# Attention with image prompts on one core: the inner products of the tokens of batches one to seven computed in four 32-column tiles of TensorE

## The chip, the cores and the metric

The kernel runs on one core of one Trainium2 chip. The metric is the device time of one execution in microseconds (us). The kernel before takes 440.3 us, the median of three executions (440.11, 440.3 and 442.06).

## The reference

Eight batches. Each has 112 query tokens of 320 channels (`hidden_states`) and 375 context tokens of 512 channels; the last 4 context tokens are image prompts, the 371 others are text. There are 20 heads of 16 channels. All is in fp32.

```python
q = heads(hidden_states @ W_q); k_t = heads(text_ehs @ W_k); v_t = heads(text_ehs @ W_v)
probs_t = softmax(q k_t^T * attn_scale)
text_out = probs_t @ v_t
attn_scores = q @ heads(ip_ehs @ W_k_ip)^T * attn_scale
qsem = l2norm(einsum('bhst,bte->bhse', probs_t, text_ehs))
sem  = einsum('bhse,bne->bhsn', qsem, l2norm(ip_ehs))
probs_ip = softmax(attn_scores + 0.5 * sem) * spatial_mask
out = (text_out + probs_ip @ heads(ip_ehs @ W_v_ip)) @ W_out + b_out + hidden_states
```

`qsem` is a vector of 512 channels for each head and query. The kernel never forms it. Its length is a quadratic form in the probabilities, with the matrix of the inner products of all text tokens with each other (the Gram matrix, 371 x 371), and its products with the prompts are the probabilities times the inner products of text and prompts. So a batch needs one matrix G of 375 columns: inner products of its tokens with its tokens, the last four columns being the normalised prompts.

## The kernel before, in words

G is symmetric, so only its upper triangle is used, with the elements off the diagonal doubled and those on it halved against that. The 375 tokens, padded to 384, are 12 blocks of 32. Block j is needed from its own first column to column 375: 375 - 32 j columns.

**The products (`gram`, L450 to L467).** `ctxT` holds the context turned round: channels on the 128 partitions, in four pieces e of 128 channels, tokens along the free dimension. For each chunk c of 128 tokens (4 blocks) four matmuls, one for each e, add up a tile of 128 tokens x (375 - 128 c) columns in a PSUM bank of its own: 375, 247 and 119 columns. The stationary operand is the chunk (128 columns), so the whole 128x128 array is used, and for three blocks in four also columns are computed that lie below the triangle. Banks come from a pool of two (`ps_mm`). `doubled` (L442) follows each chunk: ScalarE writes twice the bank into `ug` in SBUF, GpSimd multiplies the square at the diagonal by a mask `half` that holds 0.5 in the 32x32 blocks at the diagonal and 1.0 elsewhere. An fp32 matmul appears in the profile as two instructions, with a weight load each, and is called two passes here: `gram` has 24 passes for a batch.

**What it feeds.** `gram_to_groups` (L469) copies each 32 rows of `ug` by DMA to the four groups of 32 partitions of the tile `u`; `placed` (L600, GpSimd) puts the values of a group of heads behind them. `multiplied` (L679 to L699) is the largest stage: for 5 groups of 4 heads in each batch and 12 blocks of tokens, matmuls on four tiles of 32 rows at once (L692), block j with 392 - 32 j columns. Then VectorE multiplies each result with the probabilities and adds up (`reduced`, L740), ScalarE copies the sums out (`value_sums`, L705).

**What sets the order.** PE, SP and VectorE run in the order in which the program text issues instructions, ScalarE too after the prologue (`manual_schedule`); GpSimd's order is chosen by the framework's scheduler until the last batch. One step (b, g) of the main loop (L1125) issues: the 48 matmuls of `multiplied`, with the scores of the group two steps on (L637) after blocks 0 and 6, their maxima (L650, VectorE), exponentials (L654, ScalarE) and DMAs of the probabilities (L663, SP), the transpose for the next step after block 2 (L673, VectorE), `value_sums`, `reduced`, `placed`, and then `between(b, g)` (L1025), which puts other work between two steps: after g = 0 the `gram` of the next batch, after g = 1 and 2 its `values` (L531) and `keys` (L497), after g = 3 and 4 keys, queries and the output of earlier batches. Batch 0 has its own `first_gram` in the prologue (L420, on `ps_qd` banks), and after its first step `prompt_projections` (L264) runs among the chunks of batch 1's `gram`: eight matmuls that write 32 partitions each, two side by side at different partitions (L273), and then three small transposes (L289).

Of the kernel before, what the change touches and what calls it, by code (L numbers as in the profile page):

```python
# [20 lines left out]
def kernel(  # L21
# [14 lines left out]
    nc = tc.nc  # L36
# [28 lines left out]
    GCOL = [sum(WC[:c]) for c in range(NT + 1)]  # L65
    GW = GCOL[NT]
    UCOL = QN * GW
    assert (H, D, NC, NT, P) == (20, 16, 3, 3, 128) and RG == 2 * D


# [12 lines left out]
    def bank(name, spare=False):  # L83

        if spare:
            return ps_sc.tile([P, 512], F32, tag="sc", name=name)
        return ps_mm.tile([P, 512], F32, tag="mm", name=name)
# [80 lines left out]
    make_identity(nc, ident)  # L168
    nc.gpsimd.memset(wq_sb[REST:, FULL, :], 0.0)

    half = const.tile([P, P], F32, tag="half", name="half")
    nc.gpsimd.memset(half, 1.0)
    for q in range(QN):
        nc.gpsimd.memset(half[q * RG : (q + 1) * RG, q * RG : (q + 1) * RG], 0.5)

    hmask = const.tile([P, HC], F32, tag="hmask", name="hmask")
    nc.vector.tensor_reduce(
# [179 lines left out]
    def begin(b):  # L357
# [12 lines left out]
        s["pvs"] = work.tile([S, H, VW], F32, tag="pvs", name=f"pvs_{b}")  # L370
        s["vip"] = work.tile([S, NIP, H, D], F32, tag="vipb", name=f"vip_{b}")

    def region(b, c):

        u = st[b]["u"].rearrange("p (q w) -> p q w", w=GW)
        return u[:, :, GCOL[c] : GCOL[c + 1]]
# [38 lines left out]
    def warm(ps, n):  # L415

        for _ in range(n):
            nc.tensor.matmul(ps[:, NC * P :], ident, ident, start=True, stop=True)

    def first_gram():  # L420

        ctxT = st[0]["ctxT"]
        banks = []
        for c in range(NT):
            banks.append(ps_qd.tile([P, 512], F32, tag="qd", name=f"ps_g_0_{c}"))
            if c == NT - 1:
                nc.gpsimd.tensor_copy(ctxT[:, :, TT:T], ipnT[:, :, :NIP])
            c0, c1 = c * P, min(c * P + P, T)
            for r in range(c + 1):
                for e in range(NE):  # L430
                    nc.tensor.matmul(
                        banks[r][:, c0 - r * P : c1 - r * P],
                        ctxT[:, e, r * P : (r + 1) * P],
                        ctxT[:, e, c0:c1],
                        start=(e == 0),
                        stop=(e == NE - 1),
                    )
                if c == NT - 1:
                    doubled(banks[r], r)
                yield  # L440

    def doubled(ps, c):  # L442

        t0 = c * P
        k = min(P, TT - t0)
        g = ug[:, GCOL[c] : GCOL[c] + T - t0]
        nc.scalar.mul(g, ps[:, : T - t0], 2.0)
        nc.gpsimd.tensor_tensor(g[:, :k], g[:, :k], half[:, :k], ALU.mult)

    def gram(b):  # L450

        ctxT = st[b]["ctxT"]

        nc.gpsimd.tensor_copy(ctxT[:, :, TT:T], ipnT[:, :, b * NIP : (b + 1) * NIP])
        for c in range(NT):
            t0 = c * P
            ps = bank(f"ps_g_{b}_{c}")
            for e in range(NE):
                nc.tensor.matmul(  # L459
                    ps[:, : T - t0],  # L460
                    ctxT[:, e, t0 : t0 + P],
                    ctxT[:, e, t0:T],
                    start=(e == 0),
                    stop=(e == NE - 1),
                )
            doubled(ps, c)
            yield  # L467

    def gram_to_groups(b, blocks):  # L469
# [130 lines left out]
    def placed(b, g, chunks=range(NT)):  # L600

        s = st[b]
        for c in chunks:
            nc.gpsimd.tensor_copy(  # L604
                region(b, c)[:, :, UV - c * P :], s["vr"][:, c * QN : (c + 1) * QN, g, :]
            )

    def prompt_logits(b):

# [69 lines left out]
    def multiplied(b, g):  # L679
        s = st[b]  # L680
        xT = s.pop(("xT", g))
        banks = []
        for a in range(GROUP):

            if b == B - 1 and g % 2 and g < NG - 1:
                banks.append(bank(f"ps_qd_{b}_{g}_{a}", spare=a > 1))
            else:
                banks.append(ps_qd.tile([P, 512], F32, tag="qd", name=f"ps_qd_{b}_{g}_{a}"))
        for j in range(BLK):
            c, q = j // QN, j % QN  # L690
            for a in range(GROUP):
                nc.tensor.matmul(  # L692
                    banks[a][:S, j * RG : UW],
                    xT[a * RG : (a + 1) * RG, j, :S],
                    region(b, c)[a * RG : (a + 1) * RG, q, q * RG :],
                    start=(j == 0),
                    stop=(j == BLK - 1),
                )
            yield  # L699
        s["qd", g] = banks  # L700
# [317 lines left out]
    def run(key, make, pieces=1):  # L1018

        if key not in gens:  # L1020
            gens[key] = make()
        for _ in range(pieces):
            next(gens[key], None)

    def between(b, g):  # L1025

        nb = b + 1
        new = nb < B


        first = [bs for bs in pairs if bs[0] == (nb if b == 0 else nb + 1)]
        rest = [bs for bs in pairs if bs[0] == nb]
        if g == 0:
            if new:
                run(("g", nb), lambda: gram(nb), 2)
            if b == 0:
                run(("pp",), prompt_projections)
            if new:
                run(("g", nb), None)
            if b == 0:  # L1040
                run(("pp",), None)
            if b > 0 and new:
                run(("f", b - 1), lambda: finish(b - 1))
        if g == 1:
            if new:
                run(("v", nb), lambda: values(nb), 2)
            for bs in first if b == 0 else ():
                run(("q", bs[0]), lambda: project_queries(bs), 3)
        if g == 2 and new:
            run(("v", nb), None)  # L1050
            run(("k", nb), lambda: keys(nb))
            for bs in first if b == 0 else ():
                run(("q", bs[0]), None)
        if g == 2 and b > 0 and new:
            run(("f", b - 1), None, 2)
        if g == 3:
            if new:
                run(("k", nb), None, 1)
            if b > 0 and new:
                run(("f", b - 1), None)  # L1060
            for bs in first if b > 0 else ():
                run(("q", bs[0]), lambda: project_queries(bs), 3)
            if b == 0:
                run(("t", b), lambda: prompt_logits(b))
            for bs in rest:
                run(("q", bs[0]), None)
        if 0 <= g - (b == 0) < NT and nb + 1 < B:
            run(("c", nb + 1), lambda: transposed_context(nb + 1))
        if g == 4:
            if b > 0 and new:  # L1070
                run(("f", b - 1), None, 2)
            if nb < B - 1:
                run(("k", nb), None, 1)
            for bs in (first if b > 0 else []) + rest:
                run(("q", bs[0]), None)
# [49 lines left out]
    for n, (b, g) in enumerate(steps[:-NG]):  # L1125
        coming = steps[n + LEAD]
        for j, _ in enumerate(multiplied(b, g)):
            for a in {0: (2, 3), 6: (0, 1)}.get(j, ()):
                scores(*coming, a)
                if j == 0:  # L1130
                    probabilities(*coming, a)
            if j == 2:
                transposed(*steps[n + 1])
                if 1 <= g <= 3:
                    gram_to_groups(b + 1, {1: (0,), 2: (2,), 3: (3,)}[g])

                if g in (1, 2) and b > 0:
                    run(("f", b - 1), None)
        value_sums(b, g)
        if g == 2 and b > 0:  # L1140
            run(("f", b - 1), None)
        for a in (0, 1):
            probabilities(*coming, a)
        if n == len(steps) - NG - 1:
            sums = shared(b, g, GROUP // 2)
            next(sums)
            reduced(b, g, 2)
        else:
            reduced(b, g)
        placed(*steps[n + 1])  # L1150
        if g == 0 and b > 1:
            run(("f", b - 2), None)
        if n == 0:
            load_next(b + 2)
        if g == NG - 1:
            load_next(b + 3)
        if g == 1:
            gram_to_groups(b + 1, (1,))
        elif g == 3:
            values_to_groups(b + 1)  # L1160
        if g == 1 and b == 0:
            run(("pp",), None)
        if (b, g) == (B - 3, 1):
            prompt_values_by_head()
        if (b, g) == (B - 2, 1):
            bd = load_prompt_values_by_head()
        if g == NG - 1 and b < B - 2:
            prompt_values(b)
        between(b, g)
        if g == 1:  # L1170
            values_to_dram(b + 1, nc.sync, 0, 2)
        if g == 2:
            values_to_dram(b + 1, nc.sync, 2)
# [145 lines left out]
```

## Time and profile before

| | |
|---|---|
| median of three executions | 440.3 us |
| profiled execution, its own time | 440.06 us |
| its span, first to last instruction | 438.3 us |
| PE busy | 97% of the span |
| VectorE, ScalarE, GpSimd busy | 74%, 43%, 25% |
| granted TensorE clock | 1.000 |
| `gram` matmuls (L459) | 168 passes, 37.6 us busy |
| `multiplied` matmuls (L692) | 3840 passes, 219.6 us busy |

How to read it: the program is a long chain of steps on PE with the other engines beside it. Busy times of PE overlap, since matmuls are pipelined and tiles work side by side, so the length of a stage is read from the start of its first instruction to the start of the next stage's first one. "Idle before" in a group's line tells how long its engine stood idle just ahead of its instructions and what ended that.

### The profile page before, as it was taken

The page shows a single profiled execution, that of the slowest core. Times are in us where ns is not written, and L with a number is a line of the kernel's source. Part 1 is how long each engine was busy: PE and PEld are TensorE (multiplying, and loading weights), DVE is VectorE, ACT ScalarE, POOL GpSimd, SP SyncE. Part 2 cuts the span into 40 slices and gives each one's busy share as a digit, 9 for nine tenths or more (in the row PEclk, how much of TensorE's full clock was granted, in tenths as well). Part 3 has the DMA queues.
Part 4 walks back from the last instruction along what each step waited for, and adds up shares of the span by engine and source line. Part 5 has one row for each costly group of instructions (what it writes and reads, how often), then busy time and mean ns, then how long its engine had stood idle before and what let it go on. Part 6 is the DMA issues. An engine that isn't in the chain of part 4 may idle for free. (4 is left out here: it accounts for less than half of the span.)

```text
span 438.3 us, 12947 instructions
## 1 busy us (share of the span) xinstructions
PE 425.3 (97%) x5017; PEld 327.1 (75%) x5017; DVE 325.2 (74%) x669; ACT 189.2 (43%) x649; POOL 110.8 (25%) x268
## 2 busy tenths in 40 slices
PE   8998999989999999999999999999999999999976
PEld 8757767878777877788777877778777887776773
DVE  3047386887797878897797977887797877878774
ACT  2253333335344353334435353323534353336783
POOL 4301201012160211511152121511133121527340
PEclk9999999999999999999999999999999999999999
DMA  7669955674645946575646846467556527553300
GB/s 239 171 183 265 207 141 153 144 180 111 171 120 137 207 120 165 127 161 126 173 119 156 193 104 169 119 151 177 131 167 145 148 85 187 139 139 108 91 3 28
DMA packets 57611, 64.22 MB, mean 146 GB/s; under 512 B 18432, under 2 KB 51576, under 8 KB 57550
## 3 DMA queue, kind: packets, MB, share of 16 engines
q1 hardware_dynamic: 56984, 62.66, 57.0%
q8 instruction: 40, 0.66, 0.7%
q10 hardware_dynamic: 566, 0.72, 0.5%
q14 instruction: 21, 0.17, 0.1%
HBM read 18.67 MB, written 5.32 MB: 55 GB/s over the span
## 5 line engine op out<-in xcount | busy, mean ns | idle before, releaser
L692 PE MATMUL ps_qd<-u,xgT 32*112 32x328 f32 (+11 forms) x3840 | 219.6, 353 | 2.2 <-DVE xgT L673 1.2
L692 PEld LDWEIGHTS ps_qd<-u,xgT 32*112 32x112 f32 x3840 | 187.1, 172 | 35.2 <-issue 9.8
L673 DVE STREAM_TRANSPOSE xgT<-xg 128x1536 f32<-128x1536 f32 (+1 forms) x45 | 119.1, 2663 | 12.2 <-DMA xg<-p 8.1
L654 ACT ACTIVATE p<-ps_s,nmx 112x371 f32<-112x371 f32 x160 | 87.3, 584 | 86.9 <-DVE nmx L650 64.2
L650 DVE TENSOR_REDUCE nmx<-ps_s 112x1 f32<-112x371 f32 x160 | 77.8, 529 | 47.4 <-PE ps_s L637 46.2
L740 DVE CUSTOM_DVE_ANT_0 junk<-ps_qd,p 112x371 f32<-112x371 f32 x148 | 80.3, 543 | 15.7 <-ACT vext L538 0.5
L637 PE MATMUL ps_s<-kT,qm 32*112 32x375 f32 (+1 forms) x320 | 67.7, 484 | 1.0 <-ACT shared L723 0.7
L604 POOL COPY u<-vr 128x64 f32<-128x64 f32 x120 | 25.9, 237 | 151.9 <-PE ps_qd L692 102.6
L531 PE MATMUL ps_v<-wv_sb,ctxT 128*128 128x384 f32 (+1 forms) x192 | 63.5, 480 | 0.0
L531 PEld LDWEIGHTS ps_v<-wv_sb,ctxT 128*128 128x128 f32 x192 | 35.2, 190 | 19.7
L497 PE MATMUL ps_k<-ctxT,wk_sb 128*128 128x371 f32 x136 | 45.9, 482 | 0.0
L705 ACT COPY pvs<-ps_qd 112x21 f32<-112x21 f32 x150 | 16.0, 189 | 65.9 <-PE ps_qd L692 65.0
L459 PE MATMUL ps_g<-ctxT 128*128 128x375 f32 (+2 forms) x168 | 37.6, 380 | 0.0
L497 PEld LDWEIGHTS ps_k<-ctxT,wk_sb 128*128 128x128 f32 x136 | 25.1, 190 | 15.3 <-issue 0.5
L459 PEld LDWEIGHTS ps_g<-ctxT 128*128 128x128 f32 x168 | 28.0, 190 | 8.8 <-issue 0.5
L637 PEld LDWEIGHTS ps_s<-kT,qm 32*112 32x112 f32 x320 | 27.0, 170 | 6.9 <-ACT kT L504 2.1
L656 ACT COPY ipl<-ps_s 112x4 f32<-112x4 f32 x140 | 23.9, 170 | 0.0
L343 DVE TENSOR_SCALAR qm<-ps_q,emask 128x224 f32<-128x224 f32 (+1 forms) x25 | 9.1, 398 | 19.1 <-PE ps_q L334 19.0
L538 ACT COPY vext<-ps_v 128x384 f32<-128x384 f32 (+1 forms) x24 | 11.2, 468 | 22.8 <-PE ps_v L531 22.8
L386 DVE STREAM_TRANSPOSE ctxT<-ct 128x512 f32<-128x512 f32 x18 | 19.9, 1104 | 0.1
L504 ACT COPY kT<-ps_k 128x371 f32<-128x371 f32 x17 | 8.0, 469 | 25.2 <-PE ps_k L497 25.2
L883 POOL TENSOR_TENSOR wv<-vip,w 112x1280 f32<-112x1280 f32 x6 | 14.8, 2468 | 15.0 <-DVE w L823 15.0
(164 smaller groups left out, 313.8 us busy)
## 6 DMA issues: line engine op xcount, KB each, us to landing
xg<-p SPq DMA_DIRECT2D x159, 162.3 KB
u<-ug SPq DMA_DIRECT2D x128, 99.0 KB
ct<-in_ctx_dram SPq DMA_DIRECT2D x24, 176.0 KB
vr<-vd SPq DMA_DIRECT2D x32, 120.0 KB
vip<-vipd SPq DMA_DIRECT2D x6, 560.0 KB
vd<-vext SPq DMA_DIRECT2D x7, 320.0 KB
vd<-vext SPq DMA_DIRECT2D x7, 160.0 KB
out_dram<-ob SPq DMA_DIRECT2D x8, 140.0 KB
```

The lines of the kernel that those rows point to most:

```text
L386: nc.vector.transpose(ctxT[:, :, c * P : (c + 1) * P].rearrange("p e (j i) -> p j e i", i=RG), ct[:, some, :].rearrange("p j (k e) -> p j ...
L459: nc.tensor.matmul(ps[:, : T - t0], ctxT[:, e, t0 : t0 + P], ctxT[:, e, t0:T], start=(e == 0), stop=(e == NE - 1),)
L497: nc.tensor.matmul(ps[:, :TT], wk_sb[:, e, i * P : (i + 1) * P], s["ctxT"][:, e, :TT], start=(e == 0), stop=(e == NE - 1),)
L531: nc.tensor.matmul(ps[:, :w], ctxT[:, e, c * P : (c + 1) * P], wv_sb[:, e, :w], start=(e == 0), stop=(e == NE - 1),)
L604: nc.gpsimd.tensor_copy(region(b, c)[:, :, UV - c * P :], s["vr"][:, c * QN : (c + 1) * QN, g, :])
L637: nc.tensor.matmul(ps[:S, :w], qm[a * RG : (a + 1) * RG, i, r, j * S : (j + 1) * S], s["kT"][a * RG : (a + 1) * RG, i, :w], start=True, st ...
L650: nc.vector.tensor_reduce(nmx, ps[:S, :TT], AX.X, ALU.max, negate=True)
L654: nc.scalar.activation(p, ps[:S, :TT], AF.Exp, bias=nmx)
L656: nc.scalar.copy(s["ipl"][:, groups[g][a], :], ps[:S, TT:T])
L673: nc.vector.transpose(xT[:, j : j + n].rearrange("p j (k q) -> p q j k", q=QN), xg[:, :, j * RG : (j + n) * RG].rearrange("p q (j k) -> p ...
L692: nc.tensor.matmul(banks[a][:S, j * RG : UW], xT[a * RG : (a + 1) * RG, j, :S], region(b, c)[a * RG : (a + 1) * RG, q, q * RG :], start=(j ...
L740: nc.vector.tensor_tensor_reduce(out=junk, in0=ps[:S, :TT], in1=s["p", g][:, a, :], scale=1.0, scalar=0.0, op0=ALU.mult, op1=ALU.add, accu ...
```

## The change

`gram` is rewritten for batches 1 to 7. The stationary operand is one block of 32 tokens instead of a chunk of 128, and the result goes to the 32 partitions of column tile q (q = 0 to 3); the moving operand starts at the block's own first column. The 12 blocks are dealt to the four tiles by a table, and the matmuls of the tiles are issued in the order of the column count at which each tile would reach them. Chunks 1 and 2 share one bank. Parts of the banks that no matmul writes are set to zero by ScalarE (`cleared`) in block 2 of the step before. The masks, `placed` and `multiplied` follow the new order of blocks. In batch 0, the second and third piece of `prompt_projections` move by one place each: behind the steps (0, 1) and (0, 2).

```diff
+    BLOCKS = [[0, 1, 2, 3], [6, 7, 4, 5], [10, 8, 11, 9]]
+    PLACE = {j: (c, q) for c, js in enumerate(BLOCKS) for q, j in enumerate(js)}
...
-    half = const.tile([P, P], F32, tag="half", name="half")
+    half = const.tile([P, NT, P], F32, tag="half", name="half")
     nc.gpsimd.memset(half, 1.0)
-    for q in range(QN):
-        nc.gpsimd.memset(half[q * RG : (q + 1) * RG, q * RG : (q + 1) * RG], 0.5)
+    for c, js in enumerate(BLOCKS):
+        for q, j in enumerate(js):
+            nc.gpsimd.memset(
+                half[q * RG : (q + 1) * RG, c, (j - c * QN) * RG : (j - c * QN + 1) * RG], 0.5
+            )
...
+    def dealt(b, c, t):
+
+        if b == 0 or c == 0:
+            return t
+        v = t.rearrange("p (a b) w -> p a b w", a=2)
+        if c == 1:
+            return v[:, ::-1]
+        return v.rearrange("p a b w -> p b a w")[:, :, ::-1]
...
+    def cleared(ps, n=1):
+
+        w = P - RG
+        o = ps.rearrange("p (x w) -> p x w", w=2 * P)[:, :n, :w]
+        nc.scalar.mul(o, half[:, :n, :w], 0.0)
...
+    def gram_banks(b):
+
+        st["ps_g", b] = ps = [bank(f"ps_g_{b}_{c}") for c in range(2)]
+        for n, t in enumerate(ps):
+            cleared(t, n + 1)
...
-        for c in range(NT):
-            t0 = c * P
-            ps = bank(f"ps_g_{b}_{c}")
-            for e in range(NE):
-                nc.tensor.matmul(
-                    ps[:, : T - t0],
-                    ctxT[:, e, t0 : t0 + P],
-                    ctxT[:, e, t0:T],
-                    start=(e == 0),
-                    stop=(e == NE - 1),
-                )
-            doubled(ps, c)
+        ps = st.pop(("ps_g", b))
+        ps.append(ps[1][:, 2 * P :])
+
+        todo = []
+        for q in range(QN):
+            begun = 0
+            for c in range(NT):
+                for e in range(NE):
+                    todo.append((begun, c, q, e))
+                    begun += T - BLOCKS[c][q] * RG
+        todo.sort()
+        first = max(n for n, (_, c, _, _) in enumerate(todo) if c == 0)
+        for n, (_, c, q, e) in enumerate(todo):
+            j = BLOCKS[c][q]
+            nc.tensor.matmul(
+                ps[c][q * RG : (q + 1) * RG, j * RG - c * P : T - c * P],
+                ctxT[:, e, j * RG : (j + 1) * RG],
+                ctxT[:, e, j * RG : T],
+                start=(e == 0),
+                stop=(e == NE - 1),
+            )
+            if n == first:
+                doubled(ps[0][:, :T], 0, half[:, 0])
+                yield
+        for c in range(1, NT):
+            doubled(ps[c][:, : T - c * P], c, half[:, c])
             yield
...
-            nc.gpsimd.tensor_copy(
-                region(b, c)[:, :, UV - c * P :], s["vr"][:, c * QN : (c + 1) * QN, g, :]
-            )
+            v = region(b, c)[:, :, UV - c * P :]
+            if b > 0 and c > 0:
+                v = v.rearrange("p (i j) d -> p i j d", i=2)
+            nc.gpsimd.tensor_copy(v, dealt(b, c, s["vr"][:, c * QN : (c + 1) * QN, g, :]))
...
-            c, q = j // QN, j % QN
+            c, q = PLACE[j] if b > 0 else (j // QN, j % QN)
...
-                    region(b, c)[a * RG : (a + 1) * RG, q, q * RG :],
+                    region(b, c)[a * RG : (a + 1) * RG, q, j * RG - c * P :],
...
-            if b == 0:
-                run(("pp",), None)
...
             if j == 2:
+                if g == 0:
+                    gram_banks(b + 1)
...
-        if g == 1 and b == 0:
+        if g in (1, 2) and b == 0:
             run(("pp",), None)
```

More of the change, by code (lines that the diff above doesn't have):

```diff
@@ L438, in first_gram, with doubled @@
                 if c == NT - 1:
-                    doubled(banks[r], r)
+                    doubled(banks[r][:, : T - r * P], r, half[:, 0])
                 yield
-    def doubled(ps, c):
+    def doubled(ps, c, mask):
         t0 = c * P
@@ L446, in doubled @@
         g = ug[:, GCOL[c] : GCOL[c] + T - t0]
-        nc.scalar.mul(g, ps[:, : T - t0], 2.0)
-        nc.gpsimd.tensor_tensor(g[:, :k], g[:, :k], half[:, :k], ALU.mult)
+        nc.scalar.mul(g, ps, 2.0)
+        nc.gpsimd.tensor_tensor(g[:, :k], g[:, :k], mask[:, :k], ALU.mult)
+    def gram_banks(b):
+        st["ps_g", b] = ps = [bank(f"ps_g_{b}_{c}") for c in range(2)]
+        for n, t in enumerate(ps):
+            cleared(t, n + 1)
     def gram(b):
```

## The prediction, as put on record before the result was known

> **What bounds the kernel now.** I read the page's busy times and groups first, then the waits of PE, then the timeline of PE around one `gram`, then those of VectorE, ScalarE and GpSimd in the same stretch. From the page:
>
> ```profile
> PE 425.3 (97%) x5017; PEld 327.1 (75%) x5017; DVE 325.2 (74%) x669; ACT 189.2 (43%) x649; POOL 110.8 (25%) x268
> L459 PE MATMUL ps_g<-ctxT 128*128 128x375 f32 (+2 forms) x168 | 37.6, 380 | 0.0
> ```
>
> PE never rests for long: all its waits in the waits view add up to 9.4 us, and the idle time before `gram` is 0.0. So a microsecond of PE time taken out of the middle comes off the end, unless another engine is then late. What one `gram` takes is read from the timeline of PE (start, length, line, shape, count): batch 2's begins at 97.60 and the next step at 102.86, 5.26 us.
>
> ```profile
> 96.29 1.38 PE L692 MATMUL ps_qd<-u,xgT 32*112 32x200 f32 x39
> 97.60 5.34 PE L459 MATMUL ps_g<-ctxT 128*128 128x375 f32 x24
> 102.86 1.22 PE L692 MATMUL ps_qd<-u,xgT 32*112 32x392 f32 x10
> ```
>
> The starts of single passes, which this view merges, lie 0.315 us apart at 375 columns, 0.207 at 247 and 0.112 at 119. Eight of each make 5.07; the other 0.19 is the load ahead of the first and the drain behind the last. The wide ones cost 0.84 ns a column. At 119 columns that would be 0.100, so the 128-column load sets the 0.112 there. Batches 2 to 7 all take 5.26 to 5.27.
>
> **PE after the change.** The table gives tile 0 blocks 0, 6, 10 (375 + 183 + 55 = 613 columns), tile 1 343 + 151 + 119 = 613, tiles 2 and 3 581 each. Four pieces e and two passes make eight times that. If four tiles stream side by side, the longest tile needs 8 x 613 x 0.84 ns = 4.12 us. Do column tiles run side by side? The trace has one case with two of them, the prompt projections after batch 0's first step:
>
> ```profile
> 45.87 2.35 PE L273 MATMUL ps_ipkv<-wip,ipT 128*32 128x320 f32 x16
> 48.15 1.15 PE L459 MATMUL ps_g<-ctxT 128*128 128x119 f32 x8
> ```
>
> Sixteen passes of 320 columns one after another would take 16 x 0.269 = 4.30; from 45.87 to 48.15 they take 2.28, which is eight times 0.269 and 0.13 over for load and drain. So two tiles run in full at once, and the switch into and out of them costs no more than that of the full array (0.19). Four tiles of columns the trace doesn't show; four tiles of rows it shows in every step, whose 52 matmuls (48 of L692 with 2592 columns a tile, 4 of L637 with 375) make 2 x 2967 x 0.84 = 4.98 us a tile when four run at once. The step of 102.86 to 108.23 takes 5.37, the difference being narrow blocks whose loads of 112 columns set the pace, and the drain. Four at once is what that row says.
>
> New length: 4.12 + 0.13 = **4.25 us**, 1.01 less than 5.26. Six batches (2 to 7): 6.1. Batch 1 has the prompt projections in the middle: 41.49 to 49.35, 7.86 us, with two switches between tile shapes. After: 4.12 + 16 passes in pairs 2.15 + 0.13 = 6.40; the three transposes (49.24 to 49.35, 0.11) come later, behind step (0, 1). 7.86 - 6.40 - 0.11 = 1.35. Together **7.4 us**.
>
> The Trainium skill speaks against this. "TensorE: Matmul & The Clock Gate", Part 3 (section "Measured speedup vs the span model"), lists 3.07 times for four row tiles and 2.38 times for three column tiles. With 3.07 the 9552 columns of all blocks (2388 x 4) would take 2 x 9552 x 0.84 / 3.07 = 5.23 us, with 0.13 of switching 5.36, a loss of 0.1 for each batch. The row of this trace says more: 19.9 us of work of single tiles in 5.37 is 3.7 for the row tiles, and 4.30 in 2.28 is 1.9 for two column tiles, both with drain and load floors counted against them. I go by the trace.
>
> **The rate of issue** is the unknown cost. `gram` grows from 24 loads and 24 passes to 96 and 96: 192 in 4.12 us, 47 per us. The window from 102.86 to 108.23 counts 105 and 104, 39 per us, though with columns, not issue, as its pace; the stretch of 96.29 to 97.60 has 39 passes and about as many loads in 1.31, some 60 per us, but short and out of what was queued. Lower bound zero; upper bound, if 39 per us is a ceiling, 192 / 39 = 4.92 instead of 4.12: 0.8 for each batch, 5.6 in all. I take 0.05 for each batch, 0.3 in all, nearest to the 60, and keep 5.6 for the range.
>
> **Beside PE.** `cleared` adds two ScalarE writes for a batch, of 96 and 192 columns. Nearest rows: the copy of 96 columns out of PSUM (L292) takes 0.24, 224 columns (L329) 0.36; so 0.57 us. They stand after the exponentials of heads 2 and 3 and ahead of the four copies of L705, where ScalarE waits for PE (ScalarE's timeline; brackets are idle time before):
>
> ```profile
> 94.87 0.15 ACT L656 COPY ipl<-ps_s 112x4 f32<-112x4 f32 x1
> 97.70 0.41 ACT L705 COPY pvs<-ps_qd 112x21 f32<-112x21 f32 x4 [2.67 <-PE ps_qd L692]
> ```
>
> 2.67 us hide 0.57. What they wait for is the last reader of the two banks, VectorE's L343 or L874 between two batches, done at 92.56 here, 2.4 us before ScalarE gets there. Were the cover gone, L705 and the exponentials behind it would be late by 0.57, at most 4.0 for seven batches. `doubled` is three ScalarE and three GpSimd instructions of the same sizes as before; two of them now come at the end together, and SP's copies of `ug` (107.49) wait for them with some 3 us to spare. `placed` reads blocks in reverse order: the same 64 elements a partition (0.24 us each), ready 1.6 to 6 us before the next step starts, from step (0, 2) on. GpSimd's eight more memsets in the prologue (0.12 to 0.15 each) and a wider first one add about 1.4 us ahead of the wait of 2.08 in front of L427. Covered, zero; 1.4 if not.
>
> **What is late next.** The step after `gram` needs the banks that VectorE's four reductions free, so a shorter `gram` has less to hide them under. VectorE's timeline, for batch 2 and for batch 7, whose VectorE work is latest:
>
> ```profile
> 100.50 0.08 DVE L740 DVE_READ_ACCUMULATOR2_ANT ss<- 112x1 f32 x1
> 104.45 0.99 DVE L650 TENSOR_REDUCE nmx<-ps_s 112x1 f32<-112x371 f32 x2 [2.41 <-PE ps_s L637]
> ```
>
> ```profile
> 353.69 0.08 DVE L740 DVE_READ_ACCUMULATOR2_ANT ss<- 112x1 f32 x1
> 356.73 1.00 DVE L650 TENSOR_REDUCE nmx<-ps_s 112x1 f32<-112x371 f32 x2 [2.63 <-PE ps_s L637]
> ```
>
> PE would come for them at 97.60 + 4.25 = 101.85 instead of 102.86: 1.27 us after the last one in batch 2. In batch 7 `gram` starts at 349.87, so at 354.12, 0.35 after 353.77. VectorE then still idles for 1.4 us before the maxima (2.41 now), so it is in step with PE again and nothing is handed on. SP, ScalarE and the transposes (ready 5 us early in these steps) move along.
>
> **Sum.** 440.06 (the profiled execution: 438.3 of span and 1.76 around it) - 7.4 + 0.3 = 433.0 us; the median of the runs shown is 0.2 above that execution, so **433.2 us**, 1.6% less.
>
> **Rivals.**
> - Issue, or GpSimd, gives part of it back. Either issue is limited at 39 per us (5.6 lost of 7.4: 438.5), or the framework, which chooses GpSimd's order by itself, puts a copy of `placed` behind a waiting instruction, as at 48.43, where GpSimd waited 8.75 us for a DMA with two copies behind it; PE, which reads the first of them 2.3 us into step (0, 1), comes 2.2 us after it now and 0.8 then. One such wait in a batch costs some 0.5 us, 3.5 in all. 435 to 438.5.
> - The tiles overlap only as the page's ratio says, or something like it: 440.3 + 0.7 = 441, no change.
> - **Slower: column tiles go two at a time at most**, all that L273 shows. Place: `gram` itself. 2 x 9552 x 0.84 / 2 = 8.02, with 0.13 8.15 us, 2.9 more than now for each batch, 20 for seven: 460 us. It decides from where fewer than 2 x 9552 x 0.84 / 5.13 = 3.1 tiles run at once on average. For it: no row with four. Against it: four row tiles run at full pace, and two column tiles show no loss at all.
> - The change doesn't do what it says: the narrow last blocks (55 and 23 columns) wait for their loads. A load of 128 columns sets 0.112 apart; a quarter of that is 0.028, above the 0.019 of the 23-column block. That tile has 32 columns less than the longest (8 x 32 x 0.84 = 0.21 us), which holds the 0.07. Nothing in the sum.
>
> **Chances.** Forecast, 432 to 434.5: 0.68. Part of it, 435 to 438.5: 0.13. No change: 0.06. Slower: 0.13. A measurement can tell about 0.5% (2.2 us) from no change; so faster 0.80, the same 0.07, slower 0.13. The range goes from 431.5 (no issue cost, a little less around `gram`) to 438.5.
>
> **What would show it.** Right: `gram` 4.2 to 4.4 us from its first start to the next step's, passes of 32 columns in fours with starts a few ns apart, VectorE's idle time before the maxima behind it about 1.4, no new wait in front of L692. Wrong: starts of the fourth tile behind the end of another, or "issue" in front of the new matmuls; PE waiting for ScalarE's `cleared`, or for GpSimd's `placed` in step (0, 1).

## The result and the profile after

The changed kernel takes 437.4 us, the median of 17 executions, beside 440.1 for the kernel before on the same chip: ratio 0.9936 (95% interval 0.9915 to 0.9957), 0.6% faster where 1.6% were forecast. The profiled execution took 438.71 (span 437.0), above the median. Two executions further down, one of experiment 1 and one of experiment 11, ran in a slower state of the chip and are left out of the times and ratios given there.

The page of the changed kernel (busy time, share and count; then groups, with idle time before them and its cause):

```profile
PE 419.8 (96%) x5521; PEld 328.5 (75%) x5521; DVE 326.6 (75%) x669; ACT 191.5 (44%) x663; POOL 111.5 (26%) x276
...
L571 PE MATMUL ps_v<-wv_sb,ctxT 128*128 128x384 f32 (+1 forms) x192 | 65.2, 489 | 2.7 <-ACT kip L297 2.7
...
L495 PE MATMUL ps_g<-ctxT 128*32 128x375 f32 (+11 forms) x672 | 30.4, 333 | 0.0
```

PE has 504 more matmul passes and 5.5 us less busy time. `gram` (L495 now) still never waits, but `values` (L571) has a wait that was not there. The timeline of PE around batch 2's `gram`:

```profile
101.58 4.34 PE L495 MATMUL ps_g<-ctxT 128*32 128x375 f32 x96
105.86 1.22 PE L733 MATMUL ps_qd<-u,xgT 32*112 32x392 f32 x10
```

101.58 to 105.86 is 4.28 us (5.26 before), with all four tiles streaming: the first passes of the four tiles start 6 to 7 ns apart. Batches 2 to 7 all take 4.27. ScalarE's `cleared` in the step before, and VectorE behind `gram`:

```profile
98.90 0.52 ACT L438 ACTIVATE ps_g<-half 128x96 f32<-128x96 f32 x2
101.68 0.41 ACT L746 COPY pvs<-ps_qd 112x21 f32<-112x21 f32 x4 [2.26 <-PE ps_qd L733]
```

```profile
104.51 0.08 DVE L781 DVE_READ_ACCUMULATOR2_ANT ss<- 112x1 f32 x1
...
107.44 1.00 DVE L691 TENSOR_REDUCE nmx<-ps_s 112x1 f32<-112x371 f32 x2 [1.33 <-PE ps_s L678]
```

`cleared` takes 0.52 us, and 2.26 us of ScalarE's rest are left behind it. VectorE's idle time before the maxima fell from 2.41 to 1.33. So each `gram` did what was forecast. Where the gain went is seen by laying the starts of all 40 steps of the two traces side by side (after minus before, us):

| start of step | difference | what lies in the stretch before it |
|---|---|---|
| (0, 0) | +0.92 | prologue |
| (0, 1) | -0.52 | batch 1's `gram` and the prompt projections: -1.44 |
| (0, 2) | +4.02 | transposes and two chunks of values: **+4.54** |
| (1, 0) | +3.99 | |
| end | -1.36 | six `gram` of -1.00 each, and +0.65 of small waits at batch borders that differ from trace to trace |

The 4.54 us are on PE's timeline behind step (0, 1), and their cause on those of VectorE and ScalarE:

```profile
54.09 0.35 PE L294 MATMUL ps_kip<-ident,ipkv 32*128 32x32 f32 x3
54.37 2.85 PE L571 MATMUL ps_v<-wv_sb,ctxT 128*128 128x384 f32 x8
59.92 4.29 PE L571 MATMUL ps_v<-wv_sb,ctxT 128*128 128x384 f32 x8 [2.71 <-ACT kip L297]
```

```profile
55.41 2.93 DVE L714 STREAM_TRANSPOSE xgT<-xg 128x1536 f32<-128x1536 f32 x1 [4.00 <-DMA xg<-p]
58.20 0.92 DVE L691 TENSOR_REDUCE nmx<-ps_s 112x1 f32<-112x371 f32 x2
```

```profile
58.71 1.03 ACT L695 ACTIVATE p<-ps_s,nmx 112x371 f32<-112x371 f32 x2 [4.01 <-DVE nmx L691]
59.63 0.24 ACT L297 COPY kip<-ps_kip 128x96 f32<-128x96 f32 x1
```

In the kernel before, the copy of that bank stood ahead of the exponentials of step (0, 1) (51.58), the transposition waited as well, and PE ran through both chunks of values (ScalarE, VectorE, PE):

```profile
49.64 0.24 ACT L292 COPY kip<-ps_kip 128x96 f32<-128x96 f32 x1
```

```profile
54.45 2.96 DVE L673 STREAM_TRANSPOSE xgT<-xg 128x1536 f32<-128x1536 f32 x1 [2.50 <-DMA ct<-in_ctx_dram]
```

```profile
54.76 5.43 PE L531 MATMUL ps_v<-wv_sb,ctxT 128*128 128x384 f32 x16
```

Read the changed kernel's lines backwards. PE's second chunk of values needs the bank that holds the three transposes. ScalarE copies that bank out at 59.63, in order behind the exponentials of step (0, 1). Those wait for VectorE's maxima, which stand in order behind the transposition for step (0, 2), and that one waited 4.00 us for the DMA of the probabilities. The chunk itself then takes 4.29 us, where the chunk ahead of it took 2.85. The windows of that stretch show why (columns: length; busy time and count of PE, weight loads, VectorE, ScalarE, GpSimd; granted clock; DMA share; GB/s):

```profile
54.37:57.22 2.85, 2.84 (x10) 1.43 (x8) 1.81 (x1) 0.33 (x4) 0.24 (x1) 1.00 0.65 119
57.22:59.92 2.70, 0.00 (x0) 0.00 (x0) 2.56 (x6) 1.21 (x4) 0.00 (x0) 0.91 0.55 150
59.92:64.05 4.13, 4.13 (x9) 2.34 (x10) 2.77 (x10) 0.33 (x1) 0.19 (x1) 0.64 0.64 152
```

While PE rests, the granted clock starts to fall, and the next chunk runs at 0.64. So in this profile a wait of 2.7 us cost 2.7 + 1.44. The 1.44 is not in every execution: seven of the 17 have a mean clock of 0.998 or more, and their median is 437.1 us, that of the ten others 437.6. What the seven lose in its place is not shown: this profile is not one of them.

### The profile page after: what moved, and what is told of

Same layout as the page of the kernel before. It is cut to its first block, busy times and chain, and to the rows that moved or that the text cites. A ratio compares the mean times of both kernels' runs of the same rounds, so it can differ in the third digit from the quotient of the medians.

```text
span 437.0 us, 13986 instructions
## 1 busy us (share of the span) xinstructions
PE 419.8 (96%) x5521; PEld 328.5 (75%) x5521; DVE 326.6 (75%) x669; ACT 191.5 (44%) x663; POOL 111.5 (26%) x276
## 5 line engine op out<-in xcount | busy, mean ns | idle before, releaser
L571 PE MATMUL ps_v<-wv_sb,ctxT 128*128 128x384 f32 (+1 forms) x192 | 65.2, 489 | 2.7 <-ACT kip L297 2.7
L571 PEld LDWEIGHTS ps_v<-wv_sb,ctxT 128*128 128x128 f32 x192 | 35.8, 194 | 23.5 <-ACT kip L297 3.3
L495 PE MATMUL ps_g<-ctxT 128*32 128x375 f32 (+11 forms) x672 | 30.4, 333 | 0.0
L495 PEld LDWEIGHTS ps_g<-ctxT 128*32 128x32 f32 x672 | 27.7, 110 | 2.0
```

The costliest lines, as they stand in the source:

```text
L495: nc.tensor.matmul(ps[c][q * RG : (q + 1) * RG, j * RG - c * P : T - c * P], ctxT[:, e, j * RG : (j + 1) * RG], ctxT[:, e, j * RG : T], st ...
L571: nc.tensor.matmul(ps[:, :w], ctxT[:, e, c * P : (c + 1) * P], wv_sb[:, e, :w], start=(e == 0), stop=(e == NE - 1),)
```

## The experiments

All have the changed kernel as a base unless said. Ratios are to the kernel before on the same chip. Theory A: the late DMA reaches PE through the moved transposes. Rival B, in most: it would be late whoever stands behind it, or the differences are scatter. Experiments 2, 5, 7 and 8 test other steps of the account, and their expectations name their own A and B.

**1. The copy ahead of the exponentials.** The second piece of the prompt projections is cut behind ScalarE's copy:

```diff
         nc.scalar.copy(kip, ps[:, : NC * N].rearrange("p (i n) -> p i n", n=N))
+        yield
+
         for i in range(NC):
...
+        if (b, g) == (0, 1):
+            run(("pp",), None)
         for a in (0, 1):
             probabilities(*coming, a)
```

> The changed kernel, but ScalarE's copy of the three small transposes (L297) stands ahead of the exponentials of step (0, 1), and VectorE's three products with it (L299) stay where they were. Theory A: of the 7.4 us forecast, some 4.5 were given back because PE's second chunk of values waits for that copy, which stands behind exponentials, maxima and a transposition that wait for a DMA, and because TensorE's clock then falls. Then the PE wait of 2.7 us ahead of the values goes, the next step starts at about 61 instead of 65.3, and the time is 4 to 4.5 us below the changed kernel: about 433.2. Rival B: the late DMA itself is the bound, whoever stands behind it; then the step (0, 2) starts as late, with the wait moved to the banks that the reductions free, and the time stays at about 437.

Measured: 434.5 us, ratio 0.9865 (0.9836 to 0.9893). The copy stands at 54.55 and the values run through; step (0, 2) starts at 60.91 instead of 65.34. VectorE's transposition still waits 3.45 us for its DMA, so rival B falls: the DMA is late, but alone it does not hold PE. A remainder is left, 0.26 us in step (0, 2), whose banks the late reductions free.

```profile
54.28 0.41 ACT L748 COPY pvs<-ps_qd 112x21 f32<-112x21 f32 x4 [2.26 <-PE ps_qd L735]
54.55 0.27 ACT L297 COPY kip<-ps_kip 128x96 f32<-128x96 f32 x1
58.18 1.03 ACT L697 ACTIVATE p<-ps_s,nmx 112x371 f32<-112x371 f32 x2 [3.35 <-DVE nmx L693]
```

**2. The masks late.** The masks of chunks 1 and 2 move to the end of the prologue:

```diff
+    masks((0,))
...
     def more_constants():
+        masks((1, 2))
```

> The changed kernel, but the masks of chunks 1 and 2 are written at the end of the prologue, so that the memset of the two large tiles (L203) starts at 3.1 us again. Theory A: the changed kernel's prologue is 0.9 us longer because VectorE's scaling of the prompts (L255, 2.22 us instead of 0.63) runs beside that memset; then L255 takes 0.6 again, the first step starts at 36.1 to 36.3 instead of 37.06, and the time is about 0.9 lower, 436.5. Rival B: the 0.9 is scatter of the first loads from one execution to the next; then L255 is long or short as it comes and the time stays at 437.4.

Measured: 437.4 us, ratio 0.9921 (0.9890 to 0.9953), not to be told from the changed kernel's 0.9936. L255 (L260 there) is short again, 0.95 us, and the first step starts at 36.50. So the blocking is as expected, but a gain in the total is not shown; more under experiment 5. The wait ahead of the second chunk of values is there again, 2.44 us.

**3. Both edits.**

> Both edits on the changed kernel. Theory A: the forecast as it was, short of what the late DMA takes at step (0, 2): 432.5, 0.983 of the kernel before; gram itself stays at 4.28. Rival B of the two single edits: about 437.

Measured: 434.5 us, ratio 0.9874 (0.9836 to 0.9912): below Rival B's 437, but 2.0 above Theory A's 432.5 and no better than the copy alone. No wait ahead of the values, `gram` 4.27. Its first step starts at 37.43 though L260 ran free, and its transposition came as late as 55.98: step (0, 2) starts and runs 1.1 us later against step (0, 1) than in the kernel before.

**4. The transposes back ahead of step (0, 1).**

```diff
             if new:
                 run(("g", nb), None)
+            if b == 0:
+                run(("pp",), None)
...
-        if g in (1, 2) and b == 0:
+        if g == 1 and b == 0:
```

> The changed kernel, but the three transposes stand behind the prompt projections again, ahead of step (0, 1), as in the kernel before. Theory A: PE then waits there for ScalarE's three copies out of the bank and the doubling behind them (48.98 to 50.18 in the changed kernel), some 1.4 us, instead of 2.7 and the slow clock later: about 434.5, between the changed kernel and the one with the copy ahead of the exponentials. Rival B: no difference to the changed kernel, 437.4.

Measured: 434.9 us, ratio 0.9867 (0.9841 to 0.9893), as expected. PE waits there 1.03 us for ScalarE's copies, and nothing waits later:

```profile
48.01 2.32 PE L278 MATMUL ps_ipkv<-wip,ipT 128*32 128x320 f32 x16
51.35 0.31 PE L294 MATMUL ps_kip<-ident,ipkv 32*128 32x32 f32 x2 [1.03 <-ACT ipkv L289]
```

**5. The kernel before with the masks alone** (the mask tile with three planes and all twelve memsets, one plane used).

> The kernel before, with nothing but the three masks and their eight more memsets in the prologue (one plane is used). Theory A: GpSimd's memset of the large tiles moves by 1.5 us, VectorE's scaling of the prompts beside it takes about 2.2 instead of 0.63, and the time rises by 0.9, to 441.0. Rival B (scatter): L250 stays near 0.63 and the time at 440.1.

Measured: 442.05 us, ratio 1.0015 (0.9990 to 1.0041): undecided. Its trace shows the collision (VectorE, then GpSimd, of this kernel; then VectorE of the kernel before):

```profile
5.63 1.95 DVE L255 TENSOR_SCALAR ipn<-ip_sb,iprn 32x512 f32<-32x512 f32 x1
```

```profile
4.54 2.70 POOL L203 MEMSET xg<- 128x1536 f32 x2
```

```profile
5.51 0.63 DVE L250 TENSOR_SCALAR ipn<-ip_sb,iprn 32x512 f32<-32x512 f32 x1
```

The memsets end at 7.24, VectorE's instruction at 7.58. In the kernel before they end at 5.81 and 6.14. In each trace in which the instruction starts before the memsets end, it ends 0.3 us behind them, whether it started at 5.15 or at 6.66; in experiment 3, where it starts behind them, it takes 0.47. The Trainium skill has a rule for this in "SBUF — State Buffer", section "Who interferes with whom": GpSimd's port pair is shared with VectorE, `tensor_scalar` can take it under conditions, and whoever comes second is blocked, not slowed. The constant 0.3 us agrees with it.

What it costs in the total differs from execution to execution. In every trace but that of experiment 4, the first step starts 29.2 to 29.3 us behind PE's transposition of the scaled prompts (L256 in the kernel before). That transposition starts at 7.7 to 8.1 us where the memsets of the large tiles come late and at 6.9 to 8.3 where they come early. So the collision holds PE only where PE would have been there sooner; 0.9 us (36.13 against 37.03 here) is the most that these traces show.

**6. The kernel before with the move of the transposes alone** (pieces two and three behind steps (0, 1) and (0, 2)).

> The kernel before, with nothing but the move of the second and third piece of the prompt projections behind steps (0, 1) and (0, 2). Theory A: PE's second chunk of values waits for the copy of the transposes as in the changed kernel, 2 to 3 us and the slow clock behind it, less about 0.3 that the place in the first step gives back: 3 to 4.5 us slower, 443.5. Rival B: without the new gram nothing waits, 440.

Measured: 442.15 us, ratio 1.0028 (1.0004 to 1.0052). Slower, but by 1.2, not by 3 to 4.5. In its profile there is no wait: the copy ends at 58.23, when PE comes for the bank. So my size fails: the move makes the wait possible, but the old `gram` and the third chunk in its old place bring PE there some 1.1 us later than in the changed kernel, and in this execution the DMA came at 53.73 instead of 55.41.

**7. The blocks not dealt** (experiment 3, with blocks q, 4 + q, 8 + q on tile q; the placing of the values follows, which this excerpt leaves out).

```diff
-    BLOCKS = [[0, 1, 2, 3], [6, 7, 4, 5], [10, 8, 11, 9]]
+    BLOCKS = [[0, 1, 2, 3], [4, 5, 6, 7], [8, 9, 10, 11]]
```

> Both edits, with the blocks not dealt: tile q has blocks q, 4 + q and 8 + q, and the placing of values is as in the kernel before. The tiles then have 741, 645, 549 and 453 columns. Theory A: the longest tile sets the length: 8 x 741 x 0.84 = 4.98 and 0.16 for load and drain, 5.14 instead of 4.28 for each gram, 0.86 more, 6 us in all: 438.5. Rival B: the sum of columns or the count of instructions sets it, both as before: 432.5.

Measured: 440.4 us, ratio 0.9977 (0.9949 to 1.0004), 5.9 above experiment 3 where 6 were worked out (the 438.5 was worked out from 432.5, which experiment 3 did not reach). One `gram` takes 97.75 to 102.89, 5.14 us, as worked out: the longest tile sets the length.

```profile
97.75 5.21 PE L497 MATMUL ps_g<-ctxT 128*32 128x375 f32 x96
102.89 1.22 PE L733 MATMUL ps_qd<-u,xgT 32*112 32x392 f32 x10
```

**8. Issued tile after tile** (experiment 3, with the sorting left out).

```diff
-        todo.sort()
```

> Both edits, but the matmuls are issued tile after tile, twelve for tile 0, then twelve for tile 1 and so on, not in the order of their starts. Theory A: a tile has 24 loads and 24 passes, and PE looks ahead only some instructions, so the tiles overlap only in part: from 4 x 4.1 = 16.4 us a gram (no overlap, 517) down to some 8 to 12. Rival B: each tile has a queue of its own as deep as needed, and the order does not matter: 432.5.

Measured: 514.4 us, ratio 1.1663 (1.1619 to 1.1706).

```profile
107.67 15.79 PE L501 MATMUL ps_g<-ctxT 128*32 128x375 f32 x96
123.39 1.22 PE L739 MATMUL ps_qd<-u,xgT 32*112 32x392 f32 x10
```

15.72 us: hardly any overlap. By the starts of single passes, which this view merges, the next tile's first pass starts 5 to 7 ns behind the fourth pass from the end of the tile before, so ahead of three passes that were issued before it, and not earlier. Tiles have no deep queues of their own: a matmul whose tile is busy holds up all but the nearest of what is issued behind it, for all tiles.

**9. The loads late.** The order of compute is the changed kernel's; W_out and the last three batches of x are loaded after step (0, 2):

```diff
-    load_channels(nc.sync, wo_sb, w_out)
...
-    nc.sync.dma_start(x_sb[:, 5:, :], x[5:].rearrange("b s c -> s b c"))
...
+        if n == 2:
+            load_channels(nc.sync, wo_sb, w_out)
+            nc.sync.dma_start(x_sb[:, 5:, :], x[5:].rearrange("b s c -> s b c"))
```

> The changed kernel, with nothing of its order of compute changed; the loads of W_out and of the last three batches of x (820 KB) are issued after step (0, 2) instead of ahead of the main loop. Theory A: the transposition for step (0, 2) waits for its DMA because those loads share the DMA engines with it; then it starts some 2 us earlier (53 instead of 55.4), the exponentials and the copy behind them come before PE's second chunk of values, nothing waits, and the time falls to about 434, as when the copy is put ahead of the exponentials. Rival B: the DMA is late for another reason (its own issue, the loads of the prompt weights or of the contexts); then the wait stays and the time is 437.

Measured: 433.2 us, ratio 0.9846 (0.9813 to 0.9879). VectorE and ScalarE:

```profile
51.69 2.96 DVE L714 STREAM_TRANSPOSE xgT<-xg 128x1536 f32<-128x1536 f32 x1 [0.30 <-DMA xg<-p]
```

```profile
55.02 1.03 ACT L695 ACTIVATE p<-ps_s,nmx 112x371 f32<-112x371 f32 x2 [0.34 <-DVE nmx L691]
55.94 0.24 ACT L297 COPY kip<-ps_kip 128x96 f32<-128x96 f32 x1
```

The transposition starts 3.7 us earlier, the copy is done at 56.2, a microsecond before PE asks for the bank (57.0), and step (0, 2) starts at 60.91.

**10. Copy, masks and loads together.**

> Copy ahead of the exponentials, masks late and loads late together. Theory A: the step (0, 2) no longer waits for the banks either, which is worth 0.7 to 1.1 us on the kernel with the first two edits: 433.5, the whole forecast. Rival B (late for another reason): as with the first two edits, 434.5.

Measured: 433.3 us, ratio 0.9837 (0.9807 to 0.9867). With the loads late, the two other edits add nothing that can be told.

**11. The changed kernel again**, beside 9 and 10.

> The changed kernel as it is, beside the two others on the same chip. Both theories: 437.4, with a second chunk of values that waits in most executions; it shows how much of the 4.5 us of its first profile is there each time.

Measured: 438.1 us, ratio 0.9957 (0.9931 to 0.9984). The profile has the wait again, 3.17 us, with the chunk behind it at a clock of 0.62:

```profile
60.77 4.45 PE L571 MATMUL ps_v<-wv_sb,ctxT 128*128 128x384 f32 x8 [3.17 <-ACT kip L297]
```

Nine of its eleven executions have a mean clock below 0.997; of the six each of experiments 9 and 10, three in all. That is a weak sign of the wait in the others: experiment 4's profile has 0.994 without it, its clock having stood at 0.50 from 29.2 to 32.6 us, ahead of its first step (38.48).

**12. The kernel before with the loads late.**

> The kernel before, with nothing but the two loads issued after step (0, 2). It tells whether the later loads are a gain of their own. Theory A: in the kernel before nothing waits for that transposition (it is ready 3.9 us before PE starts the step), so the time stays at 440.1, and what the loads gain on the changed kernel is only what its move of the transposes had lost. Rival C: the loads hold back the kernel before as well; then it gets 1 to 4 us faster, and the change itself is worth that much less.

Measured: 440.1 us, ratio 0.9982 (0.9959 to 1.0004). The transposition no longer waits, and nothing gets faster for it:

```profile
51.88 2.96 DVE L673 STREAM_TRANSPOSE xgT<-xg 128x1536 f32<-128x1536 f32 x1
```

The loads are no gain of their own that can be told, at most 0.4%. What they gain on the changed kernel, 1.1% between experiments 11 and 9, is what the change had lost.

## Why the prediction was right and wrong

**Right.** Four column tiles run side by side. `gram` takes 4.27 us where 4.25 and 0.05 for issue were forecast; six times 1.00 and 1.44 in batch 1 make 7.4, or 7.2 with the 0.28 of the moved transposes counted, where the forecast had 7.4 less 0.3 for issue. The figure of the Trainium skill that I weighed ("TensorE: Matmul & The Clock Gate", Part 3, 3.07 times) is for four row tiles; four column tiles reach more here: 15.72 us tile after tile against 4.27 is 3.7 times. Issue at 45 instructions per us (192 in 4.27) costs nothing that can be seen. `cleared` lies under ScalarE's rest (0.52 us, 0.57 forecast), VectorE's slack shrank as worked out (1.33, 1.4 forecast), and the longest tile sets the length (experiment 7).

**Wrong: the moved step.** "The three transposes (49.24 to 49.35, 0.11) come later, behind step (0, 1)": I priced what PE does in them and not the copy that ScalarE makes of them, nor the queue that this copy was moved behind. In its new place it stands behind two exponentials, these behind two maxima, these behind a transposition that waits for a DMA; and the bank is wanted by the next work of PE but one. The chain's first link was in the trace of before, where the same transposition waited 2.50 us (put down there to another DMA). It was ready 3.9 us before PE needed its result, and the prediction let such transposes "move along" without asking who else stood behind this one. Price in the profile: 0.28 for the transposes, 2.70 of rest, 1.44 of slow clock, against the 0.11 that the sum had. Experiments 1, 4 and 9 take it away at three different links and each brings the time to 433 to 435.

**Wrong: the memsets, "covered, zero; 1.4 if not".** The cover that I named was GpSimd's own wait. What I didn't ask is who runs beside the memsets that are pushed back: VectorE's scaling, which then is blocked until they end (2.22 us instead of 0.63). The collision is in every trace with the memsets pushed back; that it costs 0.9 us in the total is not shown (experiments 2 and 5).

**The rival** "issue, or GpSimd, gives part of it back" had the outcome and the neighbourhood right (an instruction behind one that waits for a DMA in the first batch, 435 to 438.5) and the engines wrong: ScalarE and VectorE, whose order is written out, not GpSimd. With the loads late the changed kernel takes 433.2 us and beats both kernels. That this is the number forecast to a tenth is luck: the forecast was for a kernel without that edit, and the first step still starts 0.9 us later than before.

**Open.** The move alone costs the kernel before 1.2 us (experiment 6), but its one profile shows no wait; that the wait comes in some of its executions only, as the DMA lands, was not shown. Nor was it shown what the executions of the changed kernel lose that have no stretch of slow clock.

## What to carry to other kernels

When a change moves a step, follow each instruction that it issues into the queue of its engine at the new place, and ask what is ahead of it there, and what is wanted behind it: a bank freed late is a wait for whoever takes it next. A transfer that is late but hidden is a debt; making its cover shorter or putting a copy behind it calls it in, and moving loads that nobody needs yet can be cheaper than changing the order. Column tiles pay in full if the longest tile is kept short and the matmuls are issued in the order in which the tiles can start them.

## What the runs showed of the hardware

- Four fp32 tiles of 128 rows x 32 columns stream at the full rate at once: 0.84 ns a column and pass each, 192 loads and passes in 4.27 us (8 x 613 x 0.84 = 4.12 for the longest tile, and 0.15).
- Across column tiles PE keeps nearly to the order of issue: in experiment 8 a tile's first pass overtook the last three passes of the tile before and no more, so the same 48 matmuls take 15.72 us tile by tile and 4.27 in turns.
- In the three profiles in which PE rests for 2.4 to 3.2 us ahead of the second chunk of values, the granted clock stands at 0.50 for 3.4 us around the end of the rest: from 2.2 us after the rest began (changed kernel, 2.71), from 3.0 after (experiment 11, 3.17), and from 1.1 us behind its end (experiment 2, 2.44). The wait then costs half as much again (2.7 and 1.44). Such a stretch also came where PE had no rest above 1.1 us in the 10 us before (experiment 4 from 29.2 us, experiment 2 from 425.7), so a rest is not all that brings it.
- A VectorE `tensor_scalar` on fp32 that starts beside a running GpSimd memset ends 0.3 us behind it: it took up to 2.48 us (experiment 9) where it takes 0.47 alone (experiment 3).
